# A deformable-attention, token-attention and mixture-of-experts kernel on one core: the expert work of a tile is cut into three parts with places of their own, and small VectorE operands move to a PSUM bank

## The chip, the cores and the metric

The kernel runs as one program on one of the eight cores of a Trainium2 chip. The metric is device time in microseconds (us) of one launch, lower is better. The engines are named as the profile names them: PE is TensorE's matrix multiplication and PEld its weight load, DVE is VectorE, ACT is ScalarE, POOL is GpSimd, and SP is the engine that issues most DMAs.

## The reference, cut to what matters

The input is 8 images of 256 channels and 32 by 32 pixels. Layer 0 is an attention with sampled keys and with a position bias from a small network; layer 1 is a sigmoid attention over the 1024 tokens of an image, then eight experts of which each token uses two.

```python
# layer 0: every one of 1024 queries against 64 sampled keys, 4 heads
bias = jnp.sign(pos) * jnp.log1p(jnp.abs(pos))          # (queries, keys, 2)
bias = jax.nn.relu(bias @ cpb_w1.T + cpb_b1)
bias = jax.nn.relu(bias @ cpb_w2.T + cpb_b2)
bias = bias @ cpb_w3.T + cpb_b3
attn = jax.nn.softmax(sim + bias, axis=-1)
...
# layer 1
t = t + attention_of(layernorm(t))                       # sigmoid scores
logits = tokens @ router_w.T                             # top 2 of 8
for e in range(8):
    h = gelu(tokens @ w1[e] + b1[e])
    out = out + combine[:, e:e + 1] * (h @ w2[e] + b2[e])
```

## The kernel before, in words

**The main loop** has 8 images (`b`) of 64 turns (`i`). The three-layer bias network is by far the largest part, and each turn does two of its steps. A turn issues, in this order: two first layers for the turn after the next (one on DVE, L469, as a maximum; one on POOL, L471, as a difference, which ACT rectifies, L476); two second layers of this turn on PE (L484, 16 records in the profile, the mark by which turns are counted here), one emptied by ACT (L490) and one by DVE (L492); in even turns the third layer of the four steps before (L511). Then come, each as a Python generator that is moved on by one step: the preparation of the next image (`side.step`: normalization, sampling), the token attention of this or the last image (`advance(mains)`: L717, L727, and for the router `route`), the experts (`mix`), and the sum of the experts' results into the output (`step(sums)`, `combine`, L982).

**The experts.** `experts(b, rt)` (L893) serves the tokens of image `b` while image `b + 2` runs. The tokens, gathered by expert, make 12 tiles of 256 rows (15 for the last image). One round `n` of its loop does: the second layer of tile n-2 (`yp`, L928, emptied by DVE into `yt`, L933, and stored by SP), the load of tile n+2's rows and of tile n's second-layer weights, the first layer of tile n-1 (`hp`, L946, whose gelu on ACT is L954), the load of tile n+1's first-layer weights, and the four transposes of tile n (`tp`, L964, copied by ACT, L966). In the kernel before a whole round is one step, and `mix(b, i)` takes it at the end of turns 24, 26 and of every odd turn from 27 to 33 and from 41 to 57; the last step is at turn 9 of the next image. In the last image and after the loop the steps follow each other faster.

**Order and buffers.** `in_order` at the end binds every engine to the order in which the program issues; nothing is reordered later, apart from the POOL stores of gathered rows. All the PE results outside the bias network's own banks (`yp`, `hp`, `tp`, and those of attention, preparation and router) share one pool of two PSUM banks, `ps_m`. The bank `still` is apart from it: ACT writes 256 columns of it (`hold`, L458), DVE reads these in L469, and DVE keeps the router's and the convolution's intermediates in `shared`, its other half.

**Terms.** Every 8 turns a new pair of operands (`ta`, `nb`) for the first layers is loaded by SP; at `n % 8 == 3` they are scaled: `ta` by ACT (L441), `nb` by DVE (L442); at `n % 8 == 4` `second` multiplies `nb` on PE (L448) and ACT writes `nc` (L453).

**Small DVE work that the change touches:** `prep` (L236; group statistics, L251 squares two values a partition), `to_query` and `finish` (token statistics `lmv`, L577 to L583), `route` (L798; top 2, counts and slots, L816 to L886).

Of the kernel before, what the change touches and what calls it, by code (L numbers as in the profile page):

```python
# [9 lines left out]
F32 = mybir.dt.float32  # L10
# [12 lines left out]
E = 8  # L23
# [80 lines left out]
def tile_conv_attn_hybrid(ctx: ExitStack, tc: tile.TileContext, x, par, qw, w1, w2_, cst, out):  # L104
# [34 lines left out]
    held_nb = still[:, 0:256].rearrange("p (s g y) -> p s g y", g=2, y=16)  # L139
    shared = still[:, 256:512]  # L140
    attending = sorting = convolving = False

# [44 lines left out]


    ncb2 = cpool.tile([P, 1], F32, name="ncb2")
    nc.vector.tensor_scalar(ncb2, par_("cb2"), -1.0, None, ALU.mult)  # L190
# [45 lines left out]
    def prep(b, xb, st):  # L236
        qp = frames[b % 2]
        stats = small.tile([P, 2, 2, 6], F32, name="stats")
        mv = small.tile([P, 2, 2], F32, name="mv")
        for k in range(2):  # L240
            for h in range(2):
                nc.vector.bn_stats(stats[:, k, h, :], xb[:, k, halves(h)])
            nc.vector.bn_aggr(mv[:, k, :], stats[:, k, :, :].rearrange("p h s -> p (h s)"))
            yield
        gm = psum("gm")
        nc.tensor.matmul(gm[:, 0:2], lhsT=cst_("gavg"), rhs=mv[:, :, 0], start=True, stop=True)
        gmean = small.tile([P, 2], F32, name="gmean")
        nc.vector.tensor_copy(gmean, gm[:, 0:2])
        dm = small.tile([P, 2], F32, name="dm")
        nc.vector.tensor_sub(dm, mv[:, :, 0], gmean)  # L250
        nc.vector.tensor_mul(dm, dm, dm)  # L251
        nc.vector.tensor_add(dm, dm, mv[:, :, 1])
        yield
        gv = psum("gv")
        nc.tensor.matmul(gv[:, 0:2], lhsT=cst_("gavg"), rhs=dm, start=True, stop=True)
        grs = small.tile([P, 2], F32, name="grs")
# [169 lines left out]
    def terms(b, k, h, part):  # L426
# [13 lines left out]
        def scale():  # L440
            nc.scalar.activation(taf, taf, AF.Identity, bias=par_("cb1"), scale=par_("w1x"))  # L441
            nc.vector.tensor_scalar(nbf, nbf, par_("w1y"), -1.0, ALU.mult, ALU.mult)  # L442

# [156 lines left out]
    def attention(b, st, o, rt):  # L600
# [8 lines left out]
        def to_query(h):  # L609
# [18 lines left out]
            yield  # L628
            mv = small.tile([P, 4, 2], F32, name="lmv")
            for u in range(4):  # L630
# [36 lines left out]
        def finish(q):  # L667
            mv = small.tile([P, 2, 2], F32, name="lmv2")
            for u in range(2):
# [128 lines left out]
    def route(lqs, rt, slots_):  # L798
# [8 lines left out]

        def part(n, size=64):
            a = shared[:, 64 * n : 64 * n + size]
            return a.rearrange("p (m e) -> p m e", e=E) if size == 64 else a  # L810

# [9 lines left out]
        def pick(name):  # L821
            m = one.tile([P, 8], F32, name="m" + name)
            nc.vector.tensor_reduce(m, lg, AX.X, ALU.max)
            eq, first = part(1), part(2, 8)
# [32 lines left out]
        )  # L857
        many = one.tile([P, E], F32, name="many")
        nc.vector.tensor_reduce(many, need, AX.X, ALU.add)
# [3 lines left out]
        nc.vector.tensor_reduce(ends[:, 1:9], part(1), AX.X, ALU.add)  # L863
        at = part(3)
        nc.vector.scalar_tensor_tensor(
# [3 lines left out]
        for c in range(2):  # L869
            nc.vector.tensor_scalar(ws[c], m1, 0.5 - c, 0.5, ALU.mult, ALU.add)  # L870
        place = one.tile([P, 2, 8], F32, name="place")
        for c, oh in enumerate((oh1, oh2)):
            nc.vector.tensor_tensor(part(1), at, oh, ALU.mult)
            nc.vector.tensor_reduce(place[:, c], part(1), AX.X, ALU.add)
        slot = held("slot", (P, 2, 8), I32)
        nc.vector.tensor_copy(slot, place)
        yield
# [4 lines left out]
        )  # L882
        whose = one.tile([P, TILES], F32, name="whose")
        nc.vector.tensor_reduce(whose, which, AX.X, ALU.add)
# [8 lines left out]
    def experts(b, rt):  # L893
# [23 lines left out]
        fetch(0)  # L917
        yield
        fetch(1)
        first[0] = weights(0, w1pool, 2 * C + 2, w1, "w1")  # L920
        yield
        for n in range(rounds + 2):
            if n >= 2:
                f2, ht = second.pop(n - 2), tokens_.pop(n - 2)
                yp = psum("yp").rearrange("p (s c) -> p s c", s=2)
                for s in range(2):
                    for f in range(2):
                        nc.tensor.matmul(  # L928
                            yp[:, s, :], lhsT=ht[:, f, s * P : (s + 1) * P],
                            rhs=f2[:, s * several // 2, f * C : (f + 1) * C], start=(f == 0), stop=(f == 1),  # L930
                        )
                yt = low("yt")
                nc.vector.tensor_tensor(yt, yp, f2[:, 0:several, 2 * C :].to_broadcast([P, 2, C]), ALU.add)  # L933
                nc.sync.dma_start(out=yv[at(n - 2), :].rearrange("(s p) c -> p s c", p=P), in_=yt)  # L934
            if n + 2 < rounds:
                fetch(n + 2)
# [20 lines left out]
            if n + 1 < rounds:  # L957
                first[n + 1] = weights(n + 1, w1pool, 2 * C + 2, w1, "w1")
            if n < rounds:
                xl = rows.pop(n)  # L960
                tp = psum("tp").rearrange("p (k i) -> p k i", k=2)
                for k in range(2):
                    for s in range(2):
                        nc.tensor.transpose(tp[:, k, s * P : (s + 1) * P], xl[:, s, k * P : (k + 1) * P], ident)  # L964
# [108 lines left out]

    def mix(b, i):
        of = mixtures[0][0] if mixtures else NB
        if of == b - 2 and b < NB - 1:
            due = i in (24, 26) or i > 26 and i % 2 and i not in (35, 37, 39, 59, 61, 63)
        elif of == b - 3:
            due = i == 9
        else:  # L1080
            due = b == NB - 1 and (i >= TURNS - 2 if of == b - 1 else of < b and i > 9 and (i % 2 or i % 3 == 0))
        if due:
            step(mixtures)

    def step(what):
        if what and next(what[0][1], what) is what:
            what.pop(0)

    for n in range(NB * TURNS):
# [46 lines left out]
        advance(mains)  # L1136
        mix(b, i)
        step(sums)
# [124 lines left out]
```

## Time and profile before

| | |
|---|---|
| median of 3 runs | 3119.95 us (3118.14 to 3121.78) |
| the profiled execution | 3118.0 us, its span 3116.2 us |
| PE busy | 2827.7 us, 91% |
| DVE, ACT, POOL busy | 1987.2, 1851.2, 1381.8 us |
| TensorE clock granted, mean | 0.976 |
| one image in the steady loop (b = 4) | 365.6 us, of which PE is busy 347.4 |
| after the main loop | the last 270.2 us, of which PE is busy 201.4 |

A group's row gives its line, engine and operation, the tiles it writes and reads, its shapes and count; after the first bar the busy time and the mean of one in ns; after the second the idle time of the engine just before it, and who ended that. In a timeline a row is: start, length, the instruction, its count, and in brackets the idle time before it with the one who ended it. The ends of matmuls are modelled, so that some waits lie inside a busy row.

### The profile page before, as it was taken

The numbers are of one execution on the slowest core, as the hardware profiler recorded it, in microseconds if no ns is written. First come the engines' busy times: TensorE is split into PE (matmuls) and PEld (weight loads), VectorE is DVE, ScalarE is ACT, GpSimd is POOL, SyncE is SP. The second block draws the span as 40 slices with busy tenths as digits, with TensorE's granted clock in tenths as the row PEclk, the third lists the DMA queues.
The fourth block names the chain that finished last, engine by engine and source line by source line (L and its number), as shares of the span: only waits on it lengthen the run. The fifth ranks groups of instructions, "written<-read, shape, count | busy, mean of one in ns | idle before, by whom it ended". The sixth has DMA issues, their size and how long they took to land. (4 is left out here: it accounts for less than half of the span.)

```text
span 3116.2 us, 51813 instructions
## 1 busy us (share of the span) xinstructions
PE 2827.7 (91%) x19592; PEld 1397.0 (45%) x19592; DVE 1987.2 (64%) x3015; ACT 1851.2 (59%) x2662; POOL 1381.8 (44%) x945
## 2 busy tenths in 40 slices
PE   3889998899999999999999999999989999988965
PEld 2223443344445453544545444454545546425754
DVE  4887668765774777566775667757775564593212
ACT  3676655765676656765566665666567566555322
POOL 2554434643454544535454353545445343371132
PEclk7999999999999999999999999999999999999988
DMA  3321111211463234622346125542246245442376
GB/s 98 92 46 35 21 28 31 73 21 35 112 180 97 45 86 110 199 52 56 99 137 188 33 53 139 146 130 41 67 120 191 58 107 168 138 99 85 111 247 220
DMA packets 428297, 311.21 MB, mean 100 GB/s; under 512 B 284432, under 2 KB 368656, under 8 KB 428048
## 3 DMA queue, kind: packets, MB, share of 16 engines
q1 hardware_dynamic: 415472, 273.14, 32.9%
q0 software_dynamic: 12288, 33.57, 3.7%
q8 instruction: 154, 2.52, 0.4%
q10 hardware_dynamic: 288, 1.20, 0.1%
q14 instruction: 95, 0.78, 0.1%
HBM read 239.93 MB, written 67.90 MB: 99 GB/s over the span
## 5 line engine op out<-in xcount | busy, mean ns | idle before, releaser
L471 POOL TENSOR_TENSOR h<-ta,nb 128x1024 f32<-128x1024 f32 x512 | 980.5, 1916 | 1138.2 <-PE h2p L484 1040.4
L484 PE MATMUL h2p<-h,pr__101 64*64 64x512 f32 x8192 | 1023.1, 610 | 89.6 <-DVE h L492 60.7
L492 DVE TENSOR_TENSOR h<-h2p,nc 128x1024 f32<-128x1024 f32 x512 | 625.5, 1222 | 439.6 <-PE h2p L484 434.1
L490 ACT ACTIVATE h<-h2p,pr__101 128x1024 f32<-128x1024 f32 x512 | 571.0, 1115 | 474.9 <-PE h2p L484 473.7
L469 DVE TENSOR_TENSOR h<-ta,still 128x1024 f32<-128x1024 f32 x512 | 620.4, 1212 | 47.3 <-ACT still L458 44.4
L476 ACT ACTIVATE h<-h 128x1024 f32<-128x1024 f32 x512 | 538.0, 1051 | 34.5 <-POOL h L471 34.1
L484 PEld LDWEIGHTS h2p<-h,pr__101 64*64 64x64 f32 x8192 | 254.8, 133 | 619.5 <-issue 290.6
L511 PE MATMUL sim<-h,pr__101 128*32 128x512 f32 x4096 | 498.6, 605 | 0.0
L511 PEld LDWEIGHTS sim<-h,pr__101 128*32 128x32 f32 x4096 | 107.7, 110 | 367.7 <-issue 367.7
L717 PE MATMUL ap<-qt,tn 128*128 128x256 f32 x1024 | 251.1, 389 | 2.6 <-DVE x L739 1.0
L954 ACT ACTIVATE ht<-hp,w 128x128 f32<-128x128 f32 (+1 forms) x366 | 108.6, 377 | 242.0 <-PE hp L946 208.6
L727 PE MATMUL vp<-tt,sg 128*128 128x256 f32 x1024 | 233.0, 381 | 3.5 <-ACT nc L453 3.3
L928 PE MATMUL yp<-w,ht 128*128 128x256 f32 x792 | 198.4, 394 | 29.2 <-ACT ht L954 6.8
L717 PEld LDWEIGHTS ap<-qt,tn 128*128 128x128 f32 x1024 | 184.6, 190 | 86.9 <-issue 41.7
L999 POOL DMA_INDIRECT gs<-ys,slot x128 | 129.0, 1008 | 208.3 <-issue 64.9
L727 PEld LDWEIGHTS vp<-tt,sg 128*128 128x128 f32 x1024 | 193.2, 190 | 36.9 <-issue 5.7
L946 PE MATMUL hp<-xg,w 128*128 128x128 f32 (+1 forms) x1464 | 198.0, 288 | 12.0 <-PE yp L928 6.0
L739 DVE TENSOR_TENSOR x<-x,vp 128x512 f32<-128x512 f32 x64 | 44.0, 688 | 246.4 <-PE vp L727 246.4
L946 PEld LDWEIGHTS hp<-xg,w 128*128 128x128 f32 x1464 | 187.3, 194 | 29.3 <-PE yp L928 10.3
L928 PEld LDWEIGHTS yp<-w,ht 128*128 128x128 f32 x792 | 145.7, 193 | 87.5 <-issue 35.2
L933 DVE TENSOR_TENSOR yt<-yp,w 128x512 f32<-128x512 f32 x99 | 68.0, 687 | 167.6 <-PE yp L928 141.6
L735 ACT ACTIVATE sg<-ap 128x512 f32<-128x512 f32 x128 | 76.4, 598 | 148.0 <-PE ap L717 136.0
(270 smaller groups left out, 2611.1 us busy)
## 6 DMA issues: line engine op xcount, KB each, us to landing
w<-in_w SPq DMA_DIRECT2D x183, 384.0 KB
w<-in_w SPq DMA_DIRECT2D x183, 257.0 KB
ta<-fd SPq DMA_DIRECT2D x128, 256.0 KB
xl<-xs SPq DMA_DIRECT2D x99, 256.0 KB
ys<-yt SPq DMA_DIRECT2D x99, 256.0 KB
nb<-fd SPq DMA_DIRECT2D x128, 128.0 KB
xb<-in_x SPq DMA_DIRECT2D x8, 1024.0 KB
x<-in_x SPq DMA_DIRECT2D x8, 1024.0 KB
```

Of the source, the lines that this page charges most:

```text
L469: nc.vector.tensor_tensor(h1, a, b, ALU.max)
L471: nc.gpsimd.tensor_tensor(h1, a, b, ALU.subtract)
L476: nc.scalar.activation(h1, h1, AF.Relu)
L484: nc.tensor.matmul(h2p[gs, r, :], lhsT=par_("w2")[rs, gs], rhs=h1[rs, g].rearrange("p y x -> p (y x)"), start=True, stop=True, tile_positi ...
L490: nc.scalar.activation(h2, h2p, AF.Relu, bias=par_("cb2"))
L492: nc.vector.tensor_tensor(h2.rearrange("p r (y x) -> p r y x", x=W), h2p.rearrange("p r (y x) -> p r y x", x=W), nc_.unsqueeze(3).to_broad ...
L511: nc.tensor.matmul(sim[32 * q : 32 * q + 32, :], lhsT=par_("z3")[:, 15 - m : 47 - m], rhs=h2s[2 * u + q // 2][:, q % 2, :], start=False, s ...
L717: nc.tensor.matmul(ap[:, u, :], lhsT=tn[:, k, m0 : m0 + P], rhs=qt[:, k, quarter(q)], start=(k == 0), stop=(k == 1),)
L727: nc.tensor.matmul(vp[:, i, :], lhsT=sgs[s][:, u, i * P : (i + 1) * P], rhs=tt[:, 2 * todo[n - 2 + s][1] + u, :], start=(s == u == i == 0) ...
L928: nc.tensor.matmul(yp[:, s, :], lhsT=ht[:, f, s * P : (s + 1) * P], rhs=f2[:, s * several // 2, f * C : (f + 1) * C], start=(f == 0), stop ...
L946: nc.tensor.matmul(hp[:, f, us], lhsT=f1[:, u, k * C + f * P : k * C + (f + 1) * P], rhs=xg[:, k, us], start=(k == 0), stop=(k == 1),)
L999: nc.gpsimd.indirect_dma_start(out=got[m][:, c, :], out_offset=None, in_=yv[:, :], in_offset=bass.IndirectOffsetOnAxis(ap=slot[:, c, m : m ...
```

## The change

Three things change.

1. **The round is cut in three.** `experts` now yields after the second layer, after the first layer with its loads, and after the transposes. `mix` is called twice a turn: with part 0 before the first layers, and with part 1 where it stood. For images 2 to 6 the second layer of tile n-2 opens an odd turn, the loads and the first layer of tile n-1 close it, and the transposes of tile n close the even turn that follows. The two row loads and the first weights that start the sequence are one step at turn 26. The last second layer opens turn 9 of the next image. In the last image and after the loop `whole` takes three parts in a row; as the first step has no more to do than loads, such a triple is transposes, second layer, first layer.
2. **Small operands of DVE** (`lmv`, `gmean`, `dm`, `first`, `many`, `place`, `whose`) move from SBUF to free columns of `still`, which is PSUM. Since two inputs of one instruction are not both taken from there, the square of `dm` gets a second copy of the difference (`away`), and the cast of `place` becomes two.
3. **The scaling of `nb`** goes from DVE to ACT, with `nw1y`, the negated weight, made once at the start.

```diff
+    tiny = [still[:, 464 + 12 * n : 476 + 12 * n] for n in range(4)]
...
+    nw1y = cpool.tile([P, 1], F32, name="nw1y")
+    nc.vector.tensor_scalar(nw1y, par_("w1y"), -1.0, None, ALU.mult)
...
+        gmean, dm = tiny[3][:, 0:2], tiny[3][:, 2:4]
...
-        nc.vector.tensor_sub(dm, mv[:, :, 0], gmean)
-        nc.vector.tensor_mul(dm, dm, dm)
-        nc.vector.tensor_add(dm, dm, mv[:, :, 1])
+        nc.vector.tensor_sub(dm, mv[:, :, 0], gm[:, 0:2])
+        away = small.tile([P, 2], F32, name="away")
+        nc.vector.tensor_sub(away, mv[:, :, 0], gm[:, 0:2])
+        nc.vector.tensor_mul(dm, dm, away)
+        nc.vector.tensor_add(mv[:, :, 1], dm, mv[:, :, 1])
...
-            nc.vector.tensor_scalar(nbf, nbf, par_("w1y"), -1.0, ALU.mult, ALU.mult)
+            nc.scalar.activation(nbf, nbf, AF.Identity, scale=nw1y)
...
-            mv = small.tile([P, 4, 2], F32, name="lmv")
+            mv = tiny[2][:, 0:8].rearrange("p (u s) -> p u s", s=2)
...
-            mv = small.tile([P, 2, 2], F32, name="lmv2")
+            mv = tiny[q % 2][:, 0:4].rearrange("p (u s) -> p u s", s=2)
...
+        def few(n, size=8):
+            return shared[:, 192 + n : 192 + n + size]
...
-        many = one.tile([P, E], F32, name="many")
+        many = few(8)
...
-        place = one.tile([P, 2, 8], F32, name="place")
+        place = tiny[2][:, 0:8], tiny[3][:, 0:8]
...
-        nc.vector.tensor_copy(slot, place)
+        for c in range(2):
+            nc.vector.tensor_copy(slot[:, c], place[c])
...
-        whose = one.tile([P, TILES], F32, name="whose")
+        whose = shared[:, 168 : 168 + TILES]
...
         fetch(0)
-        yield
         fetch(1)
...
                 nc.sync.dma_start(out=yv[at(n - 2), :].rearrange("(s p) c -> p s c", p=P), in_=yt)
+            if n == rounds + 1:
+                break
+            yield
             if n + 2 < rounds:
                 fetch(n + 2)
...
                 first[n + 1] = weights(n + 1, w1pool, 2 * C + 2, w1, "w1")
+            yield
             if n < rounds:
                 xl = rows.pop(n)
...
-            if n < rounds + 1:
-                yield
+            yield
...
+    def mix(b, i, part):
         of = mixtures[0][0] if mixtures else NB
-        if of == b - 2 and b < NB - 1:
-            due = i in (24, 26) or i > 26 and i % 2 and i not in (35, 37, 39, 59, 61, 63)
-        elif of == b - 3:
-            due = i == 9
-        else:
-            due = b == NB - 1 and (i >= TURNS - 2 if of == b - 1 else of < b and i > 9 and (i % 2 or i % 3 == 0))
-        if due:
+        if b == NB - 1 and of >= b - 2:
+            if part and (i >= TURNS - 2 if of == b - 1 else i > 9 and (i % 2 or i % 3 == 0)):
+                whole()
+        elif of == b - 2:
+            if not part:
+                due = i in ODD
+            else:
+                due = i == 26 or i in ODD or i - 1 in ODD
+            if due:
+                step(mixtures)
+        elif of == b - 3 and i == 9 and not part:
             step(mixtures)
+
+    ODD = (27, 29, 31, 33, 41, 43, 45, 47, 49, 51, 53, 55, 57)
...
+    def whole():
+        of = mixtures[0][0] if mixtures else NB
+        for _ in range(3):
+            if mixtures and mixtures[0][0] == of:
+                step(mixtures)
...
+        mix(b, i, 0)
         new = []
...
         advance(mains)
-        mix(b, i)
+        mix(b, i, 1)
...
         if sorted_ or not attending and n % 2:
-            step(mixtures)
+            whole()
...
     while mixtures:
-        step(mixtures)
+        whole()
         step(sums)
```

More of the change, by code (lines that the diff above doesn't have):

```diff
@@ L246, in prep @@
         nc.tensor.matmul(gm[:, 0:2], lhsT=cst_("gavg"), rhs=mv[:, :, 0], start=True, stop=True)
-        gmean = small.tile([P, 2], F32, name="gmean")
         nc.vector.tensor_copy(gmean, gm[:, 0:2])
-        dm = small.tile([P, 2], F32, name="dm")
-        nc.vector.tensor_sub(dm, mv[:, :, 0], gmean)
-        nc.vector.tensor_mul(dm, dm, dm)
-        nc.vector.tensor_add(dm, dm, mv[:, :, 1])
+        nc.vector.tensor_sub(dm, mv[:, :, 0], gm[:, 0:2])
[3 more added lines that the diff above has]
+        nc.vector.tensor_add(mv[:, :, 1], dm, mv[:, :, 1])
         yield
         gv = psum("gv")
-        nc.tensor.matmul(gv[:, 0:2], lhsT=cst_("gavg"), rhs=dm, start=True, stop=True)
+        nc.tensor.matmul(gv[:, 0:2], lhsT=cst_("gavg"), rhs=mv[:, :, 1], start=True, stop=True)
         grs = small.tile([P, 2], F32, name="grs")
@@ L806, in route, with part @@
         assert not convolving
-        def part(n, size=64):
-            a = shared[:, 64 * n : 64 * n + size]
-            return a.rearrange("p (m e) -> p m e", e=E) if size == 64 else a
+        def part(n):
+            return shared[:, 64 * n : 64 * n + 64].rearrange("p (m e) -> p m e", e=E)
+        def few(n, size=8):
+            return shared[:, 192 + n : 192 + n + size]
         bank = psum("lp")
@@ L823, in pick @@
             nc.vector.tensor_reduce(m, lg, AX.X, ALU.max)
-            eq, first = part(1), part(2, 8)
+            eq, first = part(1), few(0)
             nc.vector.tensor_tensor(eq, lg, wide(m), ALU.is_equal)
@@ L863, in route @@
         nc.vector.tensor_reduce(ends[:, 1:9], part(1), AX.X, ALU.add)
-        at = part(3)
+        at = part(2)
         nc.vector.scalar_tensor_tensor(
@@ L870, in route @@
             nc.vector.tensor_scalar(ws[c], m1, 0.5 - c, 0.5, ALU.mult, ALU.add)
-        place = one.tile([P, 2, 8], F32, name="place")
+        place = tiny[2][:, 0:8], tiny[3][:, 0:8]
         for c, oh in enumerate((oh1, oh2)):
             nc.vector.tensor_tensor(part(1), at, oh, ALU.mult)
-            nc.vector.tensor_reduce(place[:, c], part(1), AX.X, ALU.add)
+            nc.vector.tensor_reduce(place[c], part(1), AX.X, ALU.add)
         slot = held("slot", (P, 2, 8), I32)
-        nc.vector.tensor_copy(slot, place)
+        for c in range(2):
+            nc.vector.tensor_copy(slot[:, c], place[c])
         yield
@@ L1070, in advance @@
                 what.remove(steps)
-    def mix(b, i):
+    def mix(b, i, part):
         of = mixtures[0][0] if mixtures else NB
-        if of == b - 2 and b < NB - 1:
-            due = i in (24, 26) or i > 26 and i % 2 and i not in (35, 37, 39, 59, 61, 63)
-        elif of == b - 3:
-            due = i == 9
-        else:
-            due = b == NB - 1 and (i >= TURNS - 2 if of == b - 1 else of < b and i > 9 and (i % 2 or i % 3 == 0))
-        if due:
+        if b == NB - 1 and of >= b - 2:
[9 more added lines that the diff above has]
+        elif of == b - 3 and i == 9 and not part:
             step(mixtures)
+    ODD = (27, 29, 31, 33, 41, 43, 45, 47, 49, 51, 53, 55, 57)
     def step(what):
```

## The prediction

> **What bounds the kernel now.** I read the page's busy shares first, then the stretches by image, then the PE timeline turn by turn.
>
> ```profile
> PE 2827.7 (91%) x19592; PEld 1397.0 (45%) x19592; DVE 1987.2 (64%) x3015; ACT 1851.2 (59%) x2662; POOL 1381.8 (44%) x945
> ```
>
> PE is in-order and nearly full: in image 4 it is busy for 347.4 of 365.6 us. No edit removes PE work, so the change can win only what PE waits: about 18 us in an image, and the waits inside modelled rows. The question is where they lie. The PE timeline of turns 49 to 53 of image 4 shows one kind:
>
> ```profile
> 1649.28 2.02 PE L946 MATMUL hp<-xg,w 128*128 128x128 f32 x16 [0.81 <-PE yp L928]
> ...
> 1664.40 0.66 PE L964 MATMUL tp<-cs,xl 128*128 128x128 f32 x4 [1.69 <-DVE yt L933]
> ...
> 1675.35 1.99 PE L928 MATMUL yp<-w,ht 128*128 128x256 f32 x8 [1.24 <-ACT xt L377]
> ```
>
> Each is the expert round asking for one of two PSUM banks in `ps_m` whose reader is late. In the second, the round wants its third bank while `yt` stands on DVE behind the softmax. Averaged over images 2 to 6, the waits that belong to the round are 0.72 us in turn 27 (transposes on the router's `un`), 1.14 in 29 (L982 on gelu), 0.10 in 31, 0.22 in 41, 0.22 in 45, 0.82 in 49, 1.84 in 51, 1.24 in 53: 6.3 us an image.
>
> The other kind is in turns 35 to 41, where the router runs. PE, then DVE, in image 4:
>
> ```profile
> 1580.94 1.09 PE L484 MATMUL h2p<-h,pr__101 64*64 64x512 f32 x8 [0.50 <-DVE h L492]
> ...
> 1586.92 1.09 PE L484 MATMUL h2p<-h,pr__101 64*64 64x512 f32 x8 [1.80 <-DVE h L492]
> ...
> 1588.67 3.45 PE L484 MATMUL h2p<-h,pr__101 64*64 64x512 f32 x16
> ```
>
> ```profile
> 1580.80 2.00 DVE L442 TENSOR_SCALAR nb<-nb,pr__101 128x512 f32<-128x512 f32 x1
> ...
> 1597.85 2.52 DVE L886 CAST expert<-whose 128x24 int32<-128x24 f32 x1
> ```
>
> DVE runs without a gap from 1577.1 to 1602.6 and PE waits for L492. A second-layer pair takes 1.95 us undisturbed; the row of 3.45 hides 1.50 of waiting. Gaps before these blocks plus their length over 1.95, in turns 36 to 41 of images 1 to 7, are 54 us. The two DVE rows are far too long for their size, as the groups show:
>
> ```profile
> L442 DVE TENSOR_SCALAR nb<-nb,pr__101 128x512 f32<-128x512 f32 x64 | 69.7, 1088 | 15.0 <-DMA nb<-fd 14.9
> L886 DVE CAST expert<-whose 128x24 int32<-128x24 f32 x8 | 10.8, 1346 | 0.3
> L251 DVE TENSOR_TENSOR dm<-dm 128x2 f32<-128x2 f32 x8 | 10.7, 1331 | 0.3
> L252 DVE TENSOR_TENSOR dm<-dm,mv 128x2 f32<-128x2 f32 x8 | 1.3, 161 | 0.3
> L607 ACT ACTIVATE x<-x,pr__101 128x512 f32<-128x512 f32 x32 | 21.1, 707 | 0.0
> ```
>
> Squaring two values takes 1331 ns on average and adding two 161. Single instances are 0.16 or 2.5 us, nothing between.
>
> **What the skill says.** The Trainium skill's "SBUF — State Buffer", section "Who interferes with whom", says that a DVE instruction with two SBUF inputs, or in a two-port mode (copy, cast, tensor_scalar), takes a port pair that it shares with GpSimd, and whoever comes second blocks for the other's whole instruction; with at most one SBUF input and outside those modes it doesn't contend. The trace agrees: the bimodal lengths, and a blocked 2.5 us fits one POOL subtraction of 1.9. The skill's "PSUM — Partial Sum Buffer", section "PSUM bank collisions raise a hardware error", has engines of one bank kept apart; the trace shows the price, 44.4 us of L469 waiting for ACT's L458 in `still`. For `nb` on ACT, "ScalarE: Activation LUTs", section "What ACT_TABLE_LOAD costs", gives 280 ns plus 0.833 ns an element, 707 ns for 512; the L607 row measures 707 at this size.
>
> **The change part by part** (against the profiled execution, 3118.0 us; the median shown is 2 us above it).
>
> *The cut round.* It is 13 rounds in each of images 2 to 6, with no instruction more: 8 records of L928 (2.0 us), 16 of L946 (1.95), 4 of L964 (0.6). Old order at the end of an odd turn: three banks in a row from a pool of two. New: transposes at the end of the even turn, second layer at the head of the odd one, first layer at its end, with a second-layer pair between. Going through the turns: at 49 the first layer takes a bank two PE pairs later, at 51 `yt` is done before the softmax, at 29 L982 no longer follows gelu: nearly all of the 6.3 us goes. Late next: transposes and second layer now ask for both banks within 0.6 us. Where the even turn's last reader is slow this waits: after L453 in turn 44 about 0.7 (in turn 52 the same wait is 0.47 and is already paid by L552), 0.1 to 0.25 in most others. I find 1.8 us an image, and take 2.8 because ACT queues may be fuller than I see. Bounds: 0, and 1.3 us a round (0.47 for the transposes, 0.85 for the second layer, as L954 makes L928 wait in the tail). Net 3.5 × 5 = **17.5 us**.
>
> Queues that it passes. DVE: `yt` (0.69) now stands before L469 (1.21) and waits for the second layer; both fit into the 1.95 of the pair that PE does next, so L492 is not later. ACT: the copy L966 (0.6) stands before the next L490, covered by the second layer's 2.0 on PE; if that cover went, 0.6 a round. Gelu with its table load is 2.4 us and now has one even turn (3.7 or more) until it is used. SP: `ys` stores move to the turn's head and wait for `yt`, with the same loads behind them as before; the `ta` and `nb` loads come in even turns and are not passed. Rows are fetched two steps at once at turn 26 and held one turn longer in `t2`; their transposes come a turn later too. Nothing on POOL moves, but the last `ys` store comes a turn earlier for its gathers.
>
> *Short operands and `nb`.* DVE work taken out of turns 35 to 41, per image, read from single rows against the short ones (0.23 for L860, 0.18 for L886): `nb` 2.0 (0.5 in image 2, 1.0 in image 7), the cast 2.3 in four images, L860 0.8 to 2.3 in four. The sum over seven images is 25.8 us. The added subtraction and second cast cost 0.3 us an image. PSUM itself I price at nothing: L827 (into PSUM) 232 ns, L823 (into SBUF) 225. Other port users stay (L844, L870, L879), and some will now meet the POOL instruction that these met, so I take two thirds: **17 us** (0 to 26).
>
> *`nb` on ACT*: 64 × 0.707 = 45 us more of ACT. It is covered where ACT waits for the matmul of L448 before L453, 43.9 us in 47 waits, 0.93 each. I take −**2 us**; without cover −45.
>
> *The last image*: with the triple turned round, L982 takes the bank of the second layer and not of gelu. There the waits are 0.99, 2.12, 0.96 and 0.80 us, and 0.82 at L946 in turn 17. I take **5 us** with what `nb` gives back in images 1 and 7 (bounds 0 and 8).
>
> *After the loop* the first triple is loads only, so image 6's experts stand two rounds further on at every step:
>
> ```profile
> 3000.04 2.46 PE L928 MATMUL yp<-w,ht 128*128 128x256 f32 x8 [2.29 <-DMA w<-in_w]
> 3006.93 1.11 PE L964 MATMUL tp<-cs,xl 128*128 128x128 f32 x4 [4.43 <-DMA xl<-xs]
> ```
>
> The last image's rows are stored by POOL until 2987.6, but their load stands in SP's queue behind image 6's last tile. That can begin 13 us earlier; about 8 us of expert work moved ahead of the router's chain takes most of it back. I take **5 us** (0 to 13).
>
> Sum: 17.5 + 17 − 2 + 5 + 5 = 42.5; 3118.0 − 42.5 = 3075.5, and with the 2 us, 3077.
>
> **The rivals.**
> - *Forecast*, 0.55: 3060 to 3095.
> - *The waits change places*: seams wait as long as the round did, and only the other 25 us come: 3095, to 3113. For it: two banks remain two. Against: between first layer and transposes a whole even turn lies. 0.20.
> - *All comes*: 26 from the port, 27 from the round, 8 and 10: 3049, with all bounds 3040. 0.08.
> - *It doesn't do what it says*: blocked port time only moves to L844, L870 and L879, and the round's waits to the seam: 3118. 0.05. The order itself is fixed by the program, so the parts do move.
> - *Slower*: at the seam both banks are asked for in 0.6 us, and the second layer, when it waits, holds up the second-layer pair behind it, which feeds ACT and DVE. Price up to 1.3 us × 65 rounds = 85 us, against 31.5 removed and 25 elsewhere: about 3147, and 3136 at 1.1 us a round. It decides from (31.5 + 25) / 65 = 0.87 us a round. Against it: no round in the timeline pays so much. 0.12.
>
> **How the numbers follow.** A measurement here can tell about 0.2%, 6 us. Faster 0.55 + 0.20 + 0.08 = 0.83, same 0.05, slower 0.12. The range 3042 to 3113 leaves out the last two cases and the edge of the third; the likeliest case alone is 3060 to 3095.
>
> **What would show it.** Right: no gap at L928, L946 and L964 in turns 49 to 53 above 0.3 us; turns 36 to 41 shorter by 2 to 4 us an image; L251 and L886 near 0.16 to 0.2 us; DVE busy down by about 90 us, ACT up by 45; PE busy unchanged with a smaller span; image 4 near 358 us. Wrong: gaps of 0.5 us or more at the transposes or the second layer in most rounds, L484 waiting for L490 in turns after `nb`, or a route whose DVE rows are long elsewhere.

## The result, and the profile after

| | before | after |
|---|---|---|
| median, runs interleaved on one chip | 3120.24 us (3116.48 to 3121.78) | 3108.98 us (3106.94 to 3115.66) |
| ratio, 95% interval | | 0.9967 (0.9957 to 0.9977) |
| the profiled execution, its span | 3118.0, 3116.2 us | 3110.18, 3108.4 us |
| image 4 | 365.6 us | 364.05 us |

The change gains 11 us. The sign was right and the time lies in the range; the gain is a quarter of the 42.5 us forecast. PE's busy time in the page is unchanged, as it was forecast:

```profile
PE 2826.4 (91%) x19592; PEld 1396.5 (45%) x19592; DVE 1911.4 (61%) x2968; ACT 1890.8 (61%) x2730; POOL 1379.2 (44%) x945
```

DVE lost 76 us (some 90 forecast), ACT gained 40 (45 forecast), PE kept its work. So the parts were done; what failed is the account of waits.

**Where the waits of the round went.** PE's waits over the whole execution (us in total, times, the longest), before and then after:

```profile
PE tp L964 <- DVE yt L933: 13.2, 13, 2.5
PE op L982 <- ACT ht L954: 11.5, 10, 2.1
```

```profile
PE tp L976 <- ACT nc L458: 8.8, 5, 1.8
PE hp L957 <- ACT xg L978: 4.4, 5, 2.2
PE hp L957 <- ACT xt L382: 3.4, 5, 0.7
```

The first two have no entry after: transposes don't wait for `yt`, and L982 not for gelu. The last three are new, and before had none of them. The PE timeline of image 4 after the change, turns 50 and 51 and then turns 44, 52 and 53:

```profile
1648.72 0.60 PE L976 MATMUL tp<-cs,xl 128*128 128x128 f32 x4
1649.56 1.99 PE L936 MATMUL yp<-w,ht 128*128 128x256 f32 x8 [0.24 <-ACT xt L382]
1651.48 1.95 PE L489 MATMUL h2p<-h,pr__101 64*64 64x512 f32 x16
1653.36 2.05 PE L957 MATMUL hp<-xg,w 128*128 128x128 f32 x16
```

```profile
1613.83 0.44 PE L453 MATMUL cp<-nb,pr__101 64*64 64x128 f32 x6 [0.47 <-ACT ht L965]
1616.03 0.66 PE L976 MATMUL tp<-cs,xl 128*128 128x128 f32 x4 [1.76 <-ACT nc L458]
...
1661.15 0.66 PE L557 MATMUL at__14421<-cs,ex 128*128 128x128 f32 x4 [1.63 <-ACT nc L458]
...
1670.59 2.05 PE L957 MATMUL hp<-xg,w 128*128 128x128 f32 x16 [0.68 <-ACT xt L382]
```

The first fence is the forecast come true: 0.24 us is left where 1.69 stood. The second is the price of the seam, as the transposes and the second layer that follows them are called here. ACT in turns 43 and 44 shows why `nc` is late:

```profile
1607.65 1.23 ACT L446 ACTIVATE ta<-ta,pr__101 128x1024 f32<-128x1024 f32 x1
1608.79 0.71 ACT L447 ACTIVATE nb<-nb,nw1y 128x512 f32<-128x512 f32 x1
...
1611.34 1.28 ACT L965 ACT_TABLE_LOAD   x1
1612.63 1.14 ACT L965 ACTIVATE ht<-hp,w 128x128 f32<-128x128 f32 x4
1613.64 1.13 ACT L495 ACTIVATE h<-h2p,pr__101 128x1024 f32<-128x1024 f32 x1
1614.64 1.08 ACT L481 ACTIVATE h<-h 128x1024 f32<-128x1024 f32 x1
1615.59 0.65 ACT L458 ACTIVATE nc<-cp,ncb 128x128 f32<-128x128 f32 x2
```

From `ta` to the end of `nc` ACT has no gap, 8.6 us long (at the dots stand L330 and L331 with a table load of their own). L453 was done at 1614.27, but ACT came to `nc` only after gelu and the turn's own L495 and L481. L453 takes both banks of `ps_m`, and only `nc` frees them. In the order before, the next to ask for one stood behind the second-layer pair of turn 45, 1.95 us of cover. Now the transposes ask for it at once, and the wait shows. It is not the work of `nb` in this queue that makes it: with `nb` back on DVE in turn 43 (below) the same wait is again 1.76 us. Of the signs that the prediction named, this is the gap of over 0.5 us at the transposes, though in some turns and not in most; and image 4 is 364 us, not near 358.

**Account by turns.** Time between the starts of turns, after minus before, from the two profiled executions (spans: −7.8 us):

| stretch | us | forecast |
|---|---|---|
| images 2 to 6, turns 26 to 36 and 42 to 58 (the round) | −9.8 + 24.2 | −17.5 |
| images 1 to 7, turns 36 to 42 (router) | −19.7 | −17 |
| images 1 to 7, turns 4 to 6 and 60 to 62 (after `nb`) | +4.2 + 3.6 | +2 for `nb` in all |
| image 7, turns 12 to 26 | +24.0 | −5 for the last image |
| images 1 to 7, turns 6 to 12 | −15.8 | 0 |
| after the loop | −5.6 | −5 |
| all else | −13.0 | 0 |

The transposes that close turn 42 instead of 41 take 0.6 us an image, 3 in all, from the router's row into the round's: without that the round is +11.3 and the router −16.7. "All else" holds the end of image 7, whose expert work now stands earlier; image 7 as a whole is +9.8.

A second profiled execution of the changed kernel shows the noise of such figures: it is 5.0 us longer in turns 42 to 58, 2.4 shorter in turns 36 to 42 and 6.5 shorter in image 7 (which is +3.3 there), and within 0.3 in turns 26 to 36, 4 to 6, 60 to 62 and 6 to 12.

Part of the differences is the TensorE clock, which falls to half for a few us at a time (see the last section). Half of such a time is lost where PE is busy, and by this estimate the 27.0 us at half clock in turns 36 to 42 of images 1 to 7 before, and 6.8 after, are worth 10 of the 16.7 us. Turns 6 to 12 had 13.7 and none, worth 7 of the 15.8; turns 42 to 58 of images 2 to 6 had none and 10.2, and 20.5 in the second execution, which fits the 5.0 between the two.

**The router.** Groups of the page's kind after (busy us, mean ns):

```profile
L447 ACT ACTIVATE nb<-nb,nw1y 128x512 f32<-128x512 f32 x64 | 45.4, 710 | 0.1
L888 DVE TENSOR_TENSOR still<-ends,cs 128x168 f32<-128x168 f32 x8 | 14.6, 1819 | 0.0
L895 DVE CAST expert<-still 128x24 int32<-128x24 f32 x8 | 1.5, 182 | 0.3
L256 DVE TENSOR_TENSOR still<-still,away 128x2 f32<-128x2 f32 x8 | 1.3, 168 | 0.3
```

The square of two values fell from 1331 to 168 ns, the cast from 1346 to 182. But the compare two instructions ahead of the cast rose. Its line before, then after (ns, least/median/most):

```profile
L879 DVE TENSOR_TENSOR still<-ends,cs x8: 330/332/2142, 536.6 to 2971.9; 128x168 f32<-128x168 f32 x8
```

```profile
L888 DVE TENSOR_TENSOR still<-ends,cs x8: 331/2246/2523, 533.7 to 2979.6; 128x168 f32<-128x168 f32 x8
```

So did the second of the three running sums in the same route, L845 before and L853 after:

```profile
L845 DVE TENSOR_TENSOR run<-run x8: 232/234/289, 524.4 to 2956.8; 128x72 f32<-128x72 f32 x8
```

```profile
L853 DVE TENSOR_TENSOR run<-run x8: 232/1822/1827, 522.1 to 2964.1; 128x72 f32<-128x72 f32 x8
```

Both still have two SBUF inputs. The compare of image 4 begins with POOL's subtraction and ends 0.2 us after it, as do the five other long compares:

```profile
1588.70 2.15 DVE L888 TENSOR_TENSOR still<-ends,cs 128x168 f32<-128x168 f32 x1
1588.71 1.92 POOL L476 TENSOR_TENSOR h<-ta,nb 128x1024 f32<-128x1024 f32 x1
```

This is in line with the Trainium skill's "SBUF — State Buffer", section "Who interferes with whom", on two SBUF inputs; the cast, whose input is in PSUM now, is 182 ns in all eight. Much of the blocked time moved to other users of the port, which is what the rival "it doesn't do what it says" held.

**After the loop**, as forecast, the experts of image 6 stand further on, and the wait for the last image's rows is one piece:

```profile
3000.30 1.12 PE L976 MATMUL tp<-cs,xl 128*128 128x128 f32 x4 [14.73 <-DMA xl<-xs]
```

### The profile page after: what moved, and what is told of

It reads as the page before. It is cut to its first block, busy times and chain, and to the rows that moved or that the text cites. A ratio compares the mean times of both kernels' runs of the same rounds, so it can differ in the third digit from the quotient of the medians.

```text
span 3108.4 us, 51840 instructions
## 1 busy us (share of the span) xinstructions
PE 2826.4 (91%) x19592; PEld 1396.5 (45%) x19592; DVE 1911.4 (61%) x2968; ACT 1890.8 (61%) x2730; POOL 1379.2 (44%) x945
## 5 line engine op out<-in xcount | busy, mean ns | idle before, releaser
L476 POOL TENSOR_TENSOR h<-ta,nb 128x1024 f32<-128x1024 f32 x512 | 979.6, 1914 | 1132.0 <-PE h2p L489 962.7
L495 ACT ACTIVATE h<-h2p,pr__101 128x1024 f32<-128x1024 f32 x512 | 570.6, 1114 | 515.9 <-PE h2p L489 514.1
L481 ACT ACTIVATE h<-h 128x1024 f32<-128x1024 f32 x512 | 538.0, 1051 | 14.2 <-POOL h L476 13.9
L957 PE MATMUL hp<-xg,w 128*128 128x128 f32 (+1 forms) x1464 | 199.9, 289 | 12.4 <-ACT xg L978 4.4
L957 PEld LDWEIGHTS hp<-xg,w 128*128 128x128 f32 x1464 | 183.3, 193 | 49.9 <-issue 29.6
```

The costliest lines, as they stand in the source:

```text
L476: nc.gpsimd.tensor_tensor(h1, a, b, ALU.subtract)
L481: nc.scalar.activation(h1, h1, AF.Relu)
L495: nc.scalar.activation(h2, h2p, AF.Relu, bias=par_("cb2"))
L957: nc.tensor.matmul(hp[:, f, us], lhsT=f1[:, u, k * C + f * P : k * C + (f + 1) * P], rhs=xg[:, k, us], start=(k == 0), stop=(k == 1),)
```

## The experiments

Ratios are to the kernel before on the same chip, with 95% intervals. "Against" compares profiled executions by turns.

### The three parts alone

Short operands alone:

> The kernel before with the short operands of DVE in PSUM alone (the round whole, nb on DVE). Port theory: the cast, the square and the product with many never block again; turns 36 to 42 lose 1.5 to 3 us an image and turns 6 to 12 some, 12 to 18 us in all: about 3105 us. Rival (the blocked time moves to nb, L844, L870 and L879): within 4 us of the kernel before, 3116 to 3120 us.

Measured: 3110.52, 0.9968 (0.9959 to 0.9977). Turns 36 to 42 give −9.0 us in seven images, all other stretches of two turns 1.7 at most. The place is the expected one; the 10.4 us in all are less than the 12 to 18 expected, and more than the rival's 4.

`nb` on ACT alone:

```diff
-            nc.vector.tensor_scalar(nbf, nbf, par_("w1y"), -1.0, ALU.mult, ALU.mult)
+            nc.scalar.activation(nbf, nbf, AF.Identity, scale=nw1y)
```

> The kernel before with the scaling of nb on ACT alone. If ACT has no cover (the prediction's -2 us was wrong): turns 4 to 6 and 60 to 62 get 0.6 us longer in every image, turns 44 to 46 and 52 to 54 by 0.5 to 1 us, 12 to 16 us in all; the router's turn 35 gives back 2 us in most images, 8 to 10 us: about 3124 us. If nb on ACT hurts only together with the cut round: 3110 us.

Measured: 3128.05, 1.0020 (1.0013 to 1.0026). Turns 4 to 6 and 60 to 62 cost 0.6 us each in nearly every image, +7.8 in all; turns 36 to 42 cost +9.1 although `nb` has left the port there, where 8 to 10 us were expected back. Turns 44 to 46 cost only +1.4, against 17.6 in the full change.

The cut round alone (the changed `experts`, `mix` and `whole`, operands and `nb` as before):

> The kernel before with the cut round alone (with its turned triple in the last image and after the loop; operands in SBUF, nb on DVE). The prediction's sum for it was 17.5 + 5 + 5 = 27.5 us gained: 3092 us. From the traces: gains of 2.4 us an image in turns 26 to 34 and 2.1 in 46 to 52, about as much lost at the seams in 42 to 46 and 52 to 58, 9 us gained by the earlier last store, 10 lost in the last image, 5 gained after the loop: about 3114 us.

Measured: 3116.56, 0.9986 (0.9978 to 0.9993). Turns 44 to 46 cost +12.2, turns 12 to 26 of image 7 +21.8, turns 26 to 34 gain about 21 in seven images, after the loop 6.9.

Medians add to −4.4 − 10.4 + 7.1 = −7.7 us, the full change has −11.3: near, but the places don't add. The router's turns have −9.0 + 9.1 − 3.6 alone (3 of the last are the transposes) and −19.7 together. I took the time by which a DVE instruction in turns 35 to 41 is longer than the shortest of its line, where it is over 0.25 us: 34.0 us before, 24.6 with short operands alone, 37.3 with `nb` alone, 28.2 after. These figures don't follow the time either: the blocked time falls most with short operands alone, the time of the turns most with all three parts. Taking one user off the port leaves the next to collide.

### `nb` on DVE again

The change with the scaling of `nb` put back:

> The changed kernel with one part undone: nb is scaled by DVE again. Theory 1 (ACT is late where nb precedes the reading of cp): the +0.6 us in turns 4 and 60 of every image goes, turns 44 and 52 lose about 1 us each, so some 20 us over seven images; against it nb blocks DVE again in the router's turn 35 (2.0 us in most images), which gives back 8 to 12 us. Sum about 3100 us (3095 to 3107). Theory 2 (the seam itself waits: transposes come straight after cp and take its bank): nb is innocent, turns 44 and 52 stay as they are, and the port comes back: 3118 us or more.

Measured: 3101.94, 0.9946 (0.9932 to 0.9959). Against the changed kernel: turns 4 to 6 −4.2, 44 to 46 −4.9, 52 to 54 −5.5, 58 to 62 −5.1; turns 6 to 12 +11.3, where `nb` in turn 11 meets POOL on the port again. The time is within the 3095 to 3107 expected; what is given back was expected in the router, which has only +2.3. What `nb` on ACT does in turn 60 shows in PE's wait for `nc` there, before, after, and with the version that follows:

```profile
PE q L654 <- ACT nc L453: 4.7, 7, 0.7
```

```profile
PE q L659 <- ACT nc L458: 9.0, 7, 1.3
```

```profile
PE q L662 <- ACT nc L461: 4.7, 7, 0.7
```

That is 0.61 us each time, most of the 0.71 us that `nb` takes.

So `nb` belongs on ACT in some turns and on DVE in others:

```diff
+            if turn in (3, 43, 51, 59):
+                nc.vector.tensor_scalar(nbf, nbf, par_("w1y"), -1.0, ALU.mult, ALU.mult)
+            else:
                 nc.scalar.activation(nbf, nbf, AF.Identity, scale=nw1y)
```

> The changed kernel with nb on DVE in turns 3, 43, 51 and 59 of an image, where ACT is read at once afterwards, and on ACT in turns 11, 19, 27 and 35. If ACT's lateness in those four turns is what nb on ACT costs, and its profit lies in the other four: turns 4 to 6, 44 to 46, 52 to 54 and 60 to 62 gain 18 us and turns 6 to 12 and 36 to 42 stay: about 3091 us. If the place of nb only shifts who meets whom at the shared port: between 3100 and 3108 us, like nb wholly on DVE.

Measured: 3092.53, 0.9903 (0.9887 to 0.9918). Against the changed kernel: −4.3, −6.7, −4.9 and −5.2 in turns 4 to 6, 44 to 46, 52 to 54 and 58 to 62, turns 6 to 12 unchanged. In images 2 to 6 that is 0.61 us in each place, but 2.2 in three of them, which are those where the changed kernel fell to half clock. This leaves the cut round by itself: in images 2 to 6, turns 26 to 36 are −9.8 and turns 42 to 58 are +13.2 against before, 9.6 of it in turns 44 to 46, +0.3 in all without the moved 3 us (+2 in a second profiled execution). The transposes of turn 44 still wait 1.76 us for `nc`.

### Both scalings a turn earlier

```diff
-            if n % 8 == 3:
+            if n % 8 == 2:
```

> The changed kernel with both scalings one turn earlier, at n % 8 == 2 in place of 3: the same ACT work, not in the turn that ends with gelu. Theory 1: ACT is on time for L458 in turns 4, 44, 52 and 60 (wait back to 0.47 us), 20 us gained: about 3090 us. Theory 2: no turn changes by more than 0.3 us: 3109 us.

Measured: 3146.9, 1.0095 (1.0080 to 1.0111), where 3090 or 3109 was expected. Where it was meant to help it did: turns 44 to 46 −12.3, 52 to 54 −6.4, 4 to 6 −4.5 and 60 to 62 −5.0 against the changed kernel. But turns 50 to 52 cost +42.7. ACT there in image 4, and then PE:

```profile
1673.09 1.24 ACT L446 ACTIVATE ta<-ta,pr__101 128x1024 f32<-128x1024 f32 x1 [3.76 <-DMA ta<-fd]
...
1677.39 0.57 ACT L382 COPY xt<-tp 128x512 f32<-128x512 f32 x1
```

```profile
1678.01 3.78 PE L936 MATMUL yp<-w,ht 128*128 128x256 f32 x8 [6.01 <-ACT xt L382]
```

ACT stands behind a load that has not landed, the copy L382 stands behind ACT, and the second layer at the seam wants the bank which that copy frees. It runs at half clock after the gap (3.78 us instead of 1.99).

### The last store at turn 9 alone

In the kernel before, only the last second layer goes to the head of turn 9:

> The kernel before, with one edit: the last second layer of an image's experts, with its store, is taken at the head of turn 9 and not at its end. If POOL's gathers wait for that store and hold the first layers up behind them, turns 6 to 12 of images 3 to 7 get 3 us shorter each, as in the changed kernel: about 3106 us. If these 3 us come from the squares and nb off the shared port, nothing changes: 3120 us.

Measured: 3115.84, 0.9984 (0.9975 to 0.9993). Turns 6 to 12 are −9.4, not the 15 expected, and turns 36 to 42, where nothing was edited, +6.7. The PE timeline before, in turn 11 of image 4, and the same step with only this edit:

```profile
1427.72 0.45 PE L246 MATMUL gm<-mv,cs 128*128 128x2 f32 x2 [2.29 <-ACT tn L647]
1428.20 5.23 PE L654 MATMUL q<-tn,qwt 128*128 128x512 f32 x8
```

```profile
1429.51 0.38 PE L246 MATMUL gm<-mv,cs 128*128 128x2 f32 x2
```

Before, the gathers wait on POOL for `ys` (the first begins 2.9 us after the store is issued, 3.2 with the edit), POOL's first layer stands behind them, ACT's L476 behind that, and `tn` behind L476. Counted from the start of turn 8, the store comes 2.5 us earlier and the first gather 2.3; that gather now goes between two first layers, and the wait of 2.29 is gone. L654 takes 5.23 us there because the clock fell to half at 1427.9, see below; with this edit the same row takes 3.74.

### The triple of the last image

```diff
-        for _ in range(3):
+        first_ = of == NB - 3 and of not in begun
+        begun.add(of)
+        for _ in range(1 if first_ else 3):
```

The first call for image 5's experts takes the loads alone, so that later triples are second layer, first layer, transposes again:

> The changed kernel, but in the last image the first call of whole takes one part alone, so that the triples of image 5's experts are second layer, first layer, transposes, as a round was before. If the turned triple makes the last image's loss of 24 us in turns 12 to 26 (its transposes and its own first layer in one call, the first layer waiting for the copy), turns 12 to 26 come back to the kernel before and the sum falls by 8 to 12 us: about 3099 us. If the loss is from the port or from nb on ACT: 3109 us, no change.

Measured: 3098.49, 0.9939 (0.9924 to 0.9953). Turns 12 to 26 of image 7 are −18.1 against the changed kernel. PE's waits in this stretch, in the changed kernel and then here:

```profile
PE at__23176 L557 <- ACT nc L458: 4.1, 1, 4.1
PE ap L722 <- ACT sg L740: 3.3, 1, 3.3
PE yp L936 <- ACT sg L740: 2.8, 2, 1.6
PE yp L936 <- ACT xg L978: 2.8, 2, 1.5
```

```profile
PE op L993 <- ACT ht L965: 3.9, 3, 2.1
PE at__23110 L557 <- ACT nc L458: 1.5, 1, 1.5
```

The wait of L993 for gelu, which the prediction wanted to save, comes back with 3.9 us and is the smaller one.

### Both repairs, and the transposes in the odd turn

Both repairs together:

> The changed kernel with both repairs together: nb scaled by DVE in turns 3, 43, 51 and 59 and by ACT in 11, 19, 27 and 35, and the first triple of image 5's experts in the last image cut to its loads, so that the triples after it are transposes last again. If the two losses are separate places (the nb one in turns 4, 44, 52, 60 of every image, the triple one in the last image), their gains add: 16.5 and 10.5 us off the changed kernel's 3109, so 3081 to 3083, 1.2% below the kernel before; turns 12 to 26 of the last image back to about +2 us against the kernel before, all other segments as with the mixed nb alone. If they share a wait (nb on ACT is part of why the turned triple is late), about 3089. If timing only drifts from one place into another: 3095 or more.

Measured: 3079.07, 0.9917 (0.9904 to 0.9931). The time is near the expected one, the ratio is not, since the kernel before took 3104.01 us on this chip. Its granted clock was a little higher there, 0.9794 on average of nine runs against 0.977 to 0.978 on the chips of the other experiments, which may be worth 5 to 7 us (an estimate, the difference times the span). What makes the rest of the 16 us stays open.

With it ran the version in which the transposes follow the first layer in the odd turn, while the second layer stays at the head:

```diff
-                due = i == 26 or i in ODD or i - 1 in ODD
+                due = i == 26 or i in ODD
             if due:
                 step(mixtures)
+                if part and i in ODD:
+                    step(mixtures)
```

> As the kernel with both repairs, but for images 2 to 6 the transposes stand at the end of the odd turn again, directly after the first layer; the second layer stays at the head of the odd turn. So the seam (transposes, then second layer, both banks within 0.6 us) is gone, and what is left of the cut is the early second layer. If the forecast gain of the cut was eaten by the seam: turns 42 to 46 and 52 to 58 lose most of the some 20 us that they gained on the kernel before (1.8 us an image in turns 44 to 46 above all, where the transposes wait for nc), turn 51 stays short because yt is still early, and of the gain in turns 26 to 30 about 1.3 us an image in turn 29 (the output transposes behind gelu) goes back; net 10 to 15 us faster than its neighbour, 3067 to 3073. If two banks with five users always wait as long, wherever the parts stand: within 4 us of its neighbour. If the early transposes were what hid gelu, the second layer waits for gelu or first layer behind them: 10 us slower.

Measured: 3084.35, 0.9935 (0.9922 to 0.9949): 5 us slower than its neighbour, where I expected 10 to 15 faster. Turns 56 to 58 (−5.7, 3 of it the moved transposes), 42 to 44, 50 to 52 and 54 to 56 (−2.5 each) do gain in images 2 to 6, but turns 26 to 30 give back 16.6 (3 of it moved transposes), not 6.5, and turns 44 to 46 stay as long (+2.2): there the second layer at the head of turn 45 asks for a late bank as the transposes did. So the seam isn't one price; each turn has its own, and none of the three outcomes that were expected is the one measured.

### The cut by place

Both repairs, and the cut only in turns 27, 29 and 51:

```diff
+            if not part:
+                parts = i == 51
+            elif i in ODD:
+                parts = 3 - (i == 51) - (i in (27, 29))
+            else:
+                parts = i in (26, 28, 30)
+            for _ in range(parts):
+                step(mixtures)
```

> Both repairs, and the cut round of images 2 to 6 only where the segments say that it pays: the transposes of turns 27 and 29 close turns 28 and 30, the second layer of turn 51 opens it; in all other odd turns the whole round stands at the end, as in the kernel before. If each place has its own price, as the segment account says (cut against whole round, images 2 to 6, in us: turns 26 to 32 -11 in all, 50 to 52 -8 to -10, everywhere else in 30 to 58 a loss, together some +20 in the version with both repairs), this is 15 to 21 us faster than the version with both repairs, 1.4 to 1.5% below the kernel before. If the losses at the seams are only what the gains turn into (a bank that comes free earlier in one turn is waited for in a later one), taking the seams away brings the old waits back in turns 41 to 49, and it is within 5 us of the version with both repairs. Turns 44 to 46 tell first: as in the kernel before, or 1.8 us an image longer.

With it, on one chip, ran the three steps that lead to it:

> The version with both repairs once more, on the chip of its neighbours, since the kernel before was 16 us shorter on the chip where it ran first. If the two repairs add: 16 us + 10 us off the changed kernel, so 9 to 11 us below the version with the mixed nb alone. If the triple costs less once nb is off ACT in turns 3, 43, 51 and 59 (the two profiles differ by only 6 us): 4 to 7 us below it.

> The version with mixed nb alone, as the measure for the version with both repairs: 0.990 of the kernel before as it was, or, if the chip decides what the port collisions cost, 0.990 to 0.995.

> The changed kernel itself on the same chip. If the gain over the kernel before is the same on every chip: ratio 0.9957 to 0.9977. If the kernel before is luckier on this chip with its port collisions (its route was not the same from run to run), the ratio is nearer 1 while the changed kernel, with fewer port users in the route, has hardly moved.

| kernel, one chip | median us | ratio (95%) |
|---|---|---|
| before | 3120.08 | |
| changed | 3110.73 | 0.9969 (0.9957 to 0.9981) |
| with mixed `nb` | 3088.32 | 0.9895 (0.9880 to 0.9910) |
| and the triple aligned | 3079.34 | 0.9873 (0.9857 to 0.9888) |
| and the cut by place | 3065.68 | 0.9828 (0.9814 to 0.9842) |

The triple is worth 9.0 us beside mixed `nb`, so the two repairs add, and the changed kernel repeats its ratio. The cut by place is 13.7 us below its neighbour, a little less than the 15 to 21 expected. Against before, in images 2 to 6, it keeps turns 26 to 32 (−10.7) and 50 to 52 (−10.3) and loses 2.9 in 52 to 54; turns 42 to 50 are as in the kernel before (within 0.3). So where the cut was taken away the old waits are back as they were (L939 on L382 five times, 6.2 us, as L928 on L377 before); they are smaller than the waits at the seams that went. The 2.9 us in turn 52 are PE's wait for `nc` at L560, 1.1 us in each image where it was 0.5. What came short is the router: turns 36 to 42 are +9.4 against the neighbour, 3 of it moved transposes. Turn 44 in image 4 now, with the transposes and the second layer out of `nc`'s way:

```profile
1598.06 0.45 PE L456 MATMUL cp<-nb,pr__101 64*64 64x128 f32 x8
1598.32 1.90 PE L492 MATMUL h2p<-h,pr__101 64*64 64x512 f32 x16
1600.15 0.33 PE L338 MATMUL fp<-cs,ft 128*128 128x128 f32 x1
1600.32 1.89 PE L939 MATMUL yp<-w,ht 128*128 128x256 f32 x8
```

## Why the prediction was right and wrong

**The cut round, 17.5 us: wrong, the net is nothing.** Both halves of the term failed. The gain was put at 6.3 us an image, "nearly all". With mixed `nb`, turns 26 to 30 gave 11.0 us (without moved transposes) and 48 to 52 gave 10.5, together 21.5 of 31.5. The waits of turns 27, 29 and 51 went as described; those of 41, 45 and 53 only changed places (1.24 at L928 became 0.68 at L957 and more at the seams). The price was put at 2.8 us an image, 14 in all, and came to 21.9. The failing sentence is "after L453 in turn 44 about 0.7": it was 1.76, since I counted `nc` as ACT's work and not what stands ahead of it on ACT: `ta`, two table loads, gelu, and last the turn's own L495 and L481. Turns 44 to 46 alone lost 9.6 us by the cut. The named rival, waits that change places, was nearest: its 3095 to 3113 holds the result.

**`nb` on ACT, −2 us: wrong.** The change without it in four turns is 22 us faster on one chip (3110.73 to 3088.32). The duration was right, 710 ns for 707. The cover was not: the average wait of 0.93 before L453 says nothing of the turns in which ACT is full. In turns 43 and 51, where gelu stands ahead of `nc`, and in 3 and 59 there is next to no cover: 0.61 us an image in each place, and 2.2 where half clock followed. Five of the ten drops of the clock in the main loop after the change lie in turns 44, 52 and 58 of images 1 to 6; with mixed `nb` that profile has none there. The bound "without cover −45" was the right end to look at.

**Short operands, 17 us: the place was right, the reason only in part.** Turns 36 to 42 gained 16.7 us. But port blocking by my measure above fell only from 34.0 to 28.2, 5.8 us; the rest of the 16.7 fits the clock, about 10 us by the estimate above. The same sum doesn't come out for short operands alone (9.4 us less blocking and about 7 less by the clock, for 9.0), so the split of the 16.7 is not settled. The two thirds taken foresaw that others would meet POOL, not that the compare L879 would take over most of L886's share (4.0 us above its shortest before, 11.9 after) and the running sum L845 8.0 us more.

**The last image, 5 us: wrong in sign.** Image 7 is 9.8 us longer (3.3 in the second profiled execution), and the aligned triple takes back 10.9 in the profile (9.0 in the medians of the last table). I followed L982 to its new bank, and not the transposes, the second layer and the first layer to theirs.

**After the loop, 5 us: right**, 5.6.

**Not in the sum: turns 6 to 12, −15.8.** The prediction has the step ("the last `ys` store comes a turn earlier for its gathers") and gives it no price. Alone it gave 9.4 there; the rest came with the other parts. In both, about half may be the clock: turns 6 to 12 had 13.7 us at half clock before, 3.4 with that edit and none after the change.

**Misread rows and a sum.** The L484 row of 3.45 us in turn 38 does not hide a wait of 1.50. The stretch in question, by windows (us, then the busy times of PE, PEld, DVE, ACT and POOL, the granted clock, DMA):

```profile
1588.30:1591.70 3.40, 3.40 (x19) 0.99 (x18) 3.23 (x8) 0.92 (x1) 0.87 (x1) 0.50 0.23 53
```

PE ran at half clock, in the stretch of 3.41 us right after one in which it had waited 1.80. So such a wait can cost nearly twice its length. Up to 13 of the 54 us counted as waits in these turns are of this kind (an estimate, half of 27.0). The blocked 2.5 us of L251 and L886 don't fit one POOL subtraction of 1.9 either: by the profile they begin 0.54 us before it and end with it. And 65 rounds at 1.1 us against 31.5 and 25 make 3133, where the prediction has 3136.

The five terms were −42.5. Measured in their places they are +0.3 for the cut, some +22 for `nb`, −16.7, +10 and −5.6, with −16 that had no term: −6 in all, with some overlap (part of `nb` lies in image 7), where the two profiles differ by −7.8.

## What to carry to other kernels

A wait removed from one user of a pair of buffers is worth what it takes in that place only; before moving a step to many places by one rule, list for each place who read the bank last and all that stands ahead of this reader on its engine. An average cover ("0.93 us in 47 waits") doesn't cover a fixed place; look at the fullest turns. When operands leave a shared port, check each remaining user of it, because the next one takes over the collision. And when two profiles are compared place by place, compare the time at half clock in each place too, before a wait is given the whole difference.

## What the runs showed of the hardware

The TensorE clock drops to half for 3.41 us (sometimes twice that) in steps of a fixed raster: in the main loop of the kernel before 13 times, after 10 times, with the cut by place 5 times. In all three, no stretch of 3.41 us on that raster with PE idle for less than 1.35 us by the profile was followed by a new drop, and none idle for more than 1.9 us escaped it; between the two it went either way. The Trainium skill's "TensorE: Matmul & The Clock Gate", section "Part 1: The HAM clock gate", gives the free-running window of about 3.4 us, and this agrees; it has the clock fall after at least one idle window, whereas here about half a window of waits was enough. A drop costs up to 1.7 us, half its length (an estimate; the 2.2 us against 0.61 in the places of `nb` are 1.6). Hence several waits of 0.5 to 1.8 us that fall into one window can cost more than they last.

A DVE instruction that meets POOL's subtraction at the shared port lasts until the subtraction has ended, here up to 0.2 us longer. So its own length says little: the compare of 168 elements takes 0.33 us alone, 1.3 when it begins 0.8 us after the subtraction, 2.1 when both begin together, and 2.5 when it begins 0.4 us ahead. By the profile's starts DVE is thus held even where it begins first, which the sentence of the prediction that "whoever comes second blocks" doesn't cover; starts on POOL are rough, and this stays open. Which instruction is hit depends on the phase against POOL and moved with the edits; turns 36 to 42 changed by 6.7 us when only the store at turn 9 was moved, where two executions of one kernel differ by 1.6 to 2.4.
